# Routing the first half of the tokens ahead of the first mixture of experts, and the rest beside its first nine tiles

## The chip, the cores and the metric

The kernel runs on one core of a Trainium2 chip. The core has a matrix engine (TensorE, PE in the profile, with its weight loads listed as PEld), three engines for elementwise work (VectorE or DVE, ScalarE or ACT, GpSimd or POOL), a queue engine (SyncE or SP) and 16 DMA engines that serve all queues. Matrix products write to PSUM, which has eight banks; everything else lies in SBUF or in DRAM. The metric is the time of one execution on the device in microseconds, less is better. Each engine works through its own instructions strictly in order, so an instruction that waits holds up all that stand behind it on its engine.

## The reference

The reference is a two-layer graph network on 4096 tokens of 256 features, in float32. Each layer adds a graph block and then a mixture of experts to its input `x`:

- Layer 0, graph block: `h = relu(adj @ layernorm(x) @ gcn_w + gcn_b)`, layer-normalised, then a selective state-space block (projection to 2 x 512, a causal convolution of width 4, `silu`, a recurrence over the 4096 tokens with 16 states for each of 512 channels, gating, projection back to 256). The sum with `x` is called x1 here.
- Layer 0, mixture: the tokens of x1 are layer-normalised; a gate of 8 columns with softmax picks the two best experts of each token, with their probabilities as weights; an expert is `gelu(t @ W1 + b1) @ W2 + b2` with 512 hidden units. The reference computes all experts for all tokens and multiplies by weights that are zero but for two; the kernel computes only the two. The sum with x1 is called x2.
- Layer 1, graph block: `tanh(adj * adj)` where `adj > 0`, at most 700 entries a row, times `tanh(layernorm(x2) @ W_proj + b_proj) @ W_gcn`, with bias and relu, added to x2. The sum is called x3.
- Layer 1, mixture: the same scheme with 6 experts of three layers and a router with a hidden layer of 128.

## The kernel before

Tokens are handled in blocks of 128 (`P`), 32 in all (`NT`), and in chunks of four blocks (`CW` = 512 tokens, `TPC` = 4), 8 in all (`NC`). The stages follow each other in the program; within all but the first a scheduler of the language orders each engine's instructions, and may take work of a later stage early where its buffers allow it.

**Graph block of layer 0.** The recurrence runs chunk after chunk; a chunk takes 32 steps, and in each step VectorE does two scans (L1115) and one product (L1125), POOL one product (L1092), ACT two exponentials (L1108), and TensorE adds up over the states (L1142). The order of this part is written out by hand (`tc.manual_schedule`). In the last chunk, beside the recurrence, the class `Norm` reads the finished chunks 0 to 6 of x1 back, normalises them, stores them to the DRAM table `dp.xd` (L945) and computes their gate logits into `lgs` (L964, L970). The class `Last` finishes chunk 7 after the recurrence: `last.norm()` (L1031 to L1066) takes its statistics from PSUM, normalises, transposes, computes logits, and stores x1 of that chunk.

**Routing of the first mixture.** The class `Dispatch` holds it for a mixture. `choose` (through `router`, L108 to L136) makes softmax and the two best experts as one-hot rows. `place` counts with two matrix products (L230, L234) how many assignments of each expert come before, and so gives each assignment a row number, kept as a high part `hi` (row divided by 128) and a low part. `one_hot` writes the low parts as one-hot matrices of 128 columns (L272, eight groups of 128 assignments an instruction; they lie in the buffer of `gn`, free by then). Each expert's rows are padded up to whole tiles of 256 rows (`TR`); with two assignments a token, 8 experts and this padding there are at most `K` = 39 tiles. `tables` turns this round into the list of tokens by row: it adds each expert's first row to `hi`, compares with the number of each half tile (L316), multiplies by group numbers (L321, and on ACT L320), and lets TensorE multiply with the one-hot matrices (L326, 64 products into one PSUM tile). From the sum VectorE derives `src` (which token to fetch, L357), then each tile's expert number `exps`, its bias columns (L364, L370) and `dst` (where to store the result, L387). Tokens are routed in two batches: 24 blocks (chunks 0 to 5) with `dp.choose(0)`, `dp.place(0)` written behind the recurrence, and 8 blocks (chunks 6 and 7) after `last.norm()`. Then `one_hot` for both, one `tables` for all 39 tiles, and after these the tiles.

**Tiles.** `expert_tiles` takes one tile after the other. SP reads the expert number into a register and loads W1 and W2 (512 KB each, three buffers, L493) and the output bias (L496); POOL fetches 256 token rows with two indirect DMAs (L392, four buffers); TensorE transposes (L500), VectorE copies (`xkT`, L504), TensorE does the first layer (L479), ACT the gelu (L483), TensorE the second layer of the tile before (L464), VectorE adds the bias (`yk`, L469), POOL stores the rows with two indirect DMAs to the DRAM table `ys` (L400). 35 tiles are always run, four more only where a count says so (the branch at L1356). Ahead of the tiles SP issues the reload of x1 into the SBUF tile `x2`, chunk by chunk (L1328, 8 x 512 KB), and four loads of layer 1's weights.

**Layer 1.** `combine` reads the results of a chunk back from `ys` and adds them to `x2`; features and propagation follow, and the second mixture, whose routing uses the same `Dispatch`, once for chunks 0 to 5 and once for chunks 6 and 7, each with its own tables. The adjacency tiles of layer 1 are loaded at L1424; the scheduler takes the first eight of these loads, and the elementwise work on them (L1430 to L1437), between tiles of the first mixture.

Of the kernel before, what the change touches and what calls it, by code (L numbers as in the profile page):

```python
# [9 lines left out]
F32 = mybir.dt.float32  # L10
# [8 lines left out]
P = 128  # L19
# [4 lines left out]
TOPK = 700  # L24
SPLIT = 6
# [3 lines left out]
def kernel(ctx: ExitStack, tc: tile.TileContext, out: bass.AP, **a):  # L29
# [131 lines left out]
    class Dispatch:  # L161
# [4 lines left out]
        def __init__(self, pool, E, name, batches, c0=0):  # L166
# [5 lines left out]
            self.C = self.K * TR // P  # L172
# [4 lines left out]
            self.src = pool.tile([P, self.C], I32, name=f"{name}_src")  # L177
            self.dst = pool.tile([P, self.C], I32, name=f"{name}_dst")
# [8 lines left out]
            self.oh, self.runs = [], []  # L187
            for T in sorted(set(batches), reverse=True):
                n = batches.count(T)
                t = pool.tile([P, n, 2 * T + 1, E], BF16, name=f"{name}_oh{T}")  # L190
                nc.gpsimd.memset(t[:, :, :1, :], 0.0)
                self.oh += [t[:, b] for b in range(n)]
                self.runs.append((t, n, T))
# [13 lines left out]
        def start(self):  # L207
            nc.gpsimd.memset(self.count, 0.0)
# [68 lines left out]
        def tables(self, ps, tp, biases, hots=None):  # L277


            E, K, C, name = self.E, self.K, self.C, self.name  # L280
# [6 lines left out]
            base = small.tile([P, 1, E], F32, name="tb_base", bufs=1)  # L287
            nc.vector.tensor_scalar(nt, self.count[:, 0, :], float(TR - 1), None, ALU.add)
            nc.vector.tensor_copy(nti, nt)
            nc.vector.tensor_scalar(nti, nti, TR.bit_length() - 1, None, ALU.arith_shift_right)  # L290
            nc.vector.tensor_copy(nt, nti)
            nc.vector.tensor_tensor_scan(ct[:, 0, :], onesf[:, :E], nt, 0.0, ALU.mult, ALU.add)
            nc.vector.tensor_tensor(base[:, 0, :], ct[:, 0, :], nt, ALU.subtract)
            nc.vector.tensor_scalar(base, base, float(TR // P), None, ALU.mult)
            self.tiles = self.pool.tile([1, 1], F32, name=f"{name}_tiles")
            nc.vector.tensor_copy(self.tiles, ct[0:1, 0, E - 1:E])

            group = self.group.rearrange("p t i -> p (t i)")
            NG = 2 * self.NT
            shift = tp.tile([P, NG], F32, name="tb_shift", bufs=1)  # L300
            g0 = 0
            for oh, n, T in self.runs:
                G, at = 2 * T, shift[:, g0:g0 + 2 * T * n].rearrange("p (n g) -> p n g", n=n)
                one = tp.tile([P, n, G, E], BF16, name=f"tb_one{G}", tag="tb_tmp", bufs=1)
                nc.vector.tensor_tensor(
                    one, oh[:, :, 1:, :], base.unsqueeze(1).to_broadcast([P, n, G, E]), ALU.mult
                )
                nc.vector.tensor_reduce(at, one, AX.X, ALU.add)
                g0 += G * n
            nc.vector.tensor_tensor(shift, shift, self.hi, ALU.add)  # L310
            yield
            S = 2 * TPC
            for g0 in range(0, NG, S):
# [3 lines left out]
                    hot, iota[:, :C].unsqueeze(1).to_broadcast([P, S, C]),  # L317
                    shift[:, g0:g0 + S].unsqueeze(2).to_broadcast([P, S, C]), ALU.is_equal,
# [6 lines left out]
                for g in range(S):  # L325
                    nc.tensor.matmul(  # L326
                        ps[:, :2 * C], self.lo[:, g0 + g, :], eq[:, :2, g, :],
# [4 lines left out]
            tmp = tp.tile([P, K, E], F32, name="tb_tmp", tag="tb_tmp", bufs=1)  # L332
            ge = tp.tile([P, K, E + 1], F32, name="tb_ge", bufs=1)
            ex = tp.tile([P, K], F32, name="tb_ex", bufs=1)
            self.exps = self.pool.tile([P, K], I32, name=f"{name}_exps")
            nc.vector.memset(ge[:, :, 0:1], 1.0)
            nc.vector.tensor_tensor(
                ge[:, :, 1:], iota[:, :K].unsqueeze(2).to_broadcast([P, K, E]),
                ct.to_broadcast([P, K, E]), ALU.is_ge,
            )  # L340
            nc.vector.tensor_reduce(ex, ge[:, :, 1:], AX.X, ALU.add)
            nc.vector.tensor_scalar(ex, ex, float(E - 1), None, ALU.min)
            nc.vector.tensor_copy(self.exps, ex)
            nc.vector.tensor_tensor(ge[:, :, :E], ge[:, :, :E], ge[:, :, 1:], ALU.subtract)
# [8 lines left out]
            nc.vector.tensor_scalar(grp, grp, self.S * TPC - 1, None, ALU.bitwise_and)  # L353
# [4 lines left out]

            yield
            self.bias = []  # L360
            for n, b in enumerate(biases):
                bk = self.pool.tile([P, b.shape[2], K], F32, name=f"{name}_b{n}")
                for m in range(b.shape[2]):
                    mul = nc.vector.tensor_tensor(  # L364
                        tmp, ge[:, :, :E],
                        b[:, :, m].unsqueeze(1).to_broadcast([P, K, E]), ALU.mult,
# [16 lines left out]
                inv[:, 1, :], inv[:, 1, :], float(2 * self.S * CW + TPC - 1), None, ALU.add  # L383
# [3 lines left out]
            nc.vector.tensor_copy(self.dst, tok)  # L387

# [8 lines left out]
        def put(self, k, yk):  # L397
            for j in range(TR // P):
                c = k * (TR // P) + j
                s_ = nc.gpsimd.indirect_dma_start(  # L400
                    out=self.ys[:, :],
# [4 lines left out]
                for o in self.sent[-3:]:  # L406
                    tc.declare_no_dep(s_.ins, o.ins, reason="distinct rows")
                if len(self.sent) > 3:
                    after(s_, self.sent[-4])
                self.sent.append(s_)  # L410
# [1307 lines left out]
```

## Time and profile before

| what | us |
|---|---|
| median of 3 runs | 2433.39 (2431.81 to 2440.27) |
| the profiled execution | 2442.82 |
| its span, first to last instruction | 2440.9 |
| TensorE busy | 2246.4 (92%) |
| VectorE busy | 1642.8 (67%) |
| ScalarE busy | 1194.4 (49%) |
| GpSimd busy | 1144.0 (47%) |
| recurrence's last product on VectorE | 1242 |
| last matrix products of x1 end | 1254 |
| list of tokens written | 1298.5 |
| first tile's transposition | 1302.4 |
| last tile's matrix products end | 1574.4 |

The page of a profile gives each engine's busy time, its busy share in 40 slices of the span, the DMA queues and the costliest groups of instructions. Matrix products are pipelined, so that a busy TensorE need not be at its peak. Other views list the instructions of an engine in order of time, with the idle time ahead of each and what ended it, or add up the busy time of all engines in a given stretch. A tile buffer's numbers are left out of its name.

### The profile page before, as it was taken

To read this page: it belongs to the slowest core of one execution; us is meant where nothing else is said; L and a number is where in the kernel's file an instruction comes from. 1 tells how busy PE (TensorE), PEld (TensorE's weight loads), DVE (VectorE), ACT (ScalarE), POOL (GpSimd) and SP (SyncE) were. 2 spreads that over 40 slices of the span, in tenths; PEclk is the share of its full clock that TensorE was granted. 3 is DMA by queue.
4 is the path that set the end of the run, shared out by engine and by line. 5 is a ranking of instruction groups with operands and counts; after the bars stand their busy time and mean duration, and the time that the engine had idled before them with its cause. 6 is when DMAs were issued, how large, how long until landed. Compare 5 with 4: busy or idle time off the path is not lost. (4 is left out here: it accounts for less than half of the span.)

```text
span 2440.9 us, 27933 instructions
## 1 busy us (share of the span) xinstructions
PE 2246.4 (92%) x8984; PEld 1628.6 (67%) x8984; DVE 1642.8 (67%) x2353; ACT 1194.4 (49%) x2045; POOL 1144.0 (47%) x831
## 2 busy tenths in 40 slices
PE   8999999999999999888966999789999999998985
PEld 7675666556565666544645888667888888877774
DVE  2079999999999999997985211191666667732133
ACT  3255566575755566675733222145555556522221
POOL 1057787777878777765623555310000000145552
PEclk9999999999999999998977999999999999999998
DMA  7289998999999998995746877551444444546686
GB/s 236 87 231 228 249 273 233 276 242 271 246 268 248 255 260 238 272 258 173 245 130 217 252 235 231 160 172 52 147 147 147 147 146 144 164 147 201 215 276 232
DMA packets 290957, 509.46 MB, mean 209 GB/s; under 512 B 25312, under 2 KB 157536, under 8 KB 289904
## 3 DMA queue, kind: packets, MB, share of 16 engines
q1 hardware_dynamic: 244528, 410.54, 53.8%
q0 software_dynamic: 46272, 97.03, 18.5%
q8 instruction: 74, 1.21, 0.2%
q14 instruction: 83, 0.68, 0.1%
HBM read 406.03 MB, written 42.73 MB: 184 GB/s over the span
## 5 line engine op out<-in xcount | busy, mean ns | idle before, releaser
L1092 POOL TENSOR_TENSOR db<-du,bb 128x1024 f32<-128x1024 f32 x256 | 607.6, 2373 | 327.1 <-ACT state L1121 80.0
L1115 DVE TENSOR_TENSOR_SCAN db<-da,state,db 128x512 f32<-128x512 f32 x512 | 627.2, 1266 | 32.2 <-ACT da L1108 30.0
L627 PE MATMUL pt<-at,gn 128*128 128x256 f32 x2048 | 479.7, 387 | 14.9 <-ACT gn L85 9.4
L627 PEld LDWEIGHTS pt<-at,gn 128*128 128x128 f32 x2048 | 396.9, 195 | 137.2 <-issue 62.9
L1108 ACT ACTIVATE da<-dt,negA 128x512 f32<-128x512 f32 x512 | 346.3, 688 | 247.8 <-DVE db L1115 237.2
L1442 PE MATMUL pf<-gn,f 128*128 128x256 f32 x2048 | 452.0, 380 | 0.0
L1442 PEld LDWEIGHTS pf<-gn,f 128*128 128x128 f32 x2048 | 386.6, 190 | 57.2 <-issue 6.4
L1125 DVE TENSOR_TENSOR hc<-db,cb 128x1024 f32<-128x1024 f32 x256 | 327.5, 1279 | 18.1 <-issue 0.4
L1142 PE MATMUL psy<-hc,ident 128*128 128x512 f32 x576 | 304.1, 623 | 4.7 <-DMA hc<-hc 4.6
L469 DVE TENSOR_TENSOR yk<-ps_y,bk 128x512 f32<-128x512 f32 x73 | 50.5, 691 | 341.7 <-PE ps_y L464 273.0
L79 POOL TENSOR_TENSOR ln_rs<-ln_rs,mhalf 128x4 f32<-128x4 f32 (+1 forms) x25 | 33.2, 1330 | 507.1 <-DVE ln_rs L78 506.7
L479 PE MATMUL ps_h<-xkT,wk 128*128 128x256 f32 x864 | 215.2, 390 | 20.6 <-DVE xkT L504 9.4
L1431 ACT ACTIVATE f<-f 128x1024 f32<-128x1024 f32 x128 | 134.6, 1057 | 202.1 <-DVE f L1430 136.8
L464 PE MATMUL ps_y<-wk,hk 128*128 128x256 f32 x864 | 214.6, 385 | 10.5 <-ACT hk L483 6.3
L479 PEld LDWEIGHTS ps_h<-xkT,wk 128*128 128x128 f32 x864 | 160.0, 193 | 57.6 <-ACT hk L483 18.5
L1129 POOL DMA_DIRECT2D hc<-hc x224 | 195.6, 873 | 0.2
L1430 DVE TENSOR_SCALAR f<-at 128x1024 f32<-128x1024 f32 x128 | 88.0, 687 | 149.3 <-PE pf L1442 134.8
L464 PEld LDWEIGHTS ps_y<-wk,hk 128*128 128x128 f32 x864 | 162.9, 193 | 34.0 <-ACT hk L483 7.7
L1142 PEld LDWEIGHTS psy<-hc,ident 128*128 128x128 f32 x576 | 110.5, 198 | 90.8 <-issue 62.1
L1437 DVE SCALAR_TENSOR_TENSOR cnt<-at,cnt 128x1024 bf16<-128x1024 f32 x120 | 146.0, 1217 | 18.4 <-DMA at<-in_adjT_dram 17.7
L483 ACT ACTIVATE hk<-ps_h,d_b 128x256 f32<-128x256 f32 x140 | 65.9, 474 | 185.8 <-PE ps_h L479 171.4
L1432 ACT ACTIVATE f<-f 128x1024 f32<-128x1024 f32 x128 | 134.5, 1055 | 3.4
(306 smaller groups left out, 2550.4 us busy)
## 6 DMA issues: line engine op xcount, KB each, us to landing
at<-in_adjT_dram SPq DMA_DIRECT2D x256, 512.0 KB
bb<-bcd SPq DMA_DIRECT2D x128, 512.0 KB
cb<-bcd SPq DMA_DIRECT2D x128, 512.0 KB
hc<-hc POOLq DMA_DIRECT2D x224, 256.0 KB
wk<-in_L_ffn_W_dram SPq DMA_DIRECT2D x70, 512.0 KB
wk<-in_L_ffn_expert_w_dram SPq DMA_DIRECT2D x114, 256.0 KB
yg<-d_ys SPq DMA_DIRECT2D x14, 512.0 KB
yd<-us SPq DMA_DIRECT2D x6, 1024.0 KB
```

What stands on the lines that cost most here:

```text
L464: nc.tensor.matmul(ps[:, j, :], hT[:, m, j * P:(j + 1) * P], w[:, m, :], start=(m == 0), stop=(m == kb_out - 1),)
L479: nc.tensor.matmul(ps[:, j, :], w[:, d, m * P:(m + 1) * P], xT[:, d, :], start=(d == 0), stop=(d == DB - 1),)
L627: nc.tensor.matmul(pt[:, k, :], xl[:, j, k * P:(k + 1) * P], at[:, jj, :], start=(j == 0 and k == 0), stop=(j == NT - 1 and k == DB - 1),)
L1092: nc.gpsimd.tensor_tensor(self.db, self.f.du[self.half][:, self.mi:self.mi + 1, :].to_broadcast([P, 2, CW]), self.bb, ALU.mult,)
L1108: nc.scalar.activation(da, self.f.dt[self.half][:, self.mi, :], AF.Exp, scale=negA[:, self.m, n:n + 1])
L1115: nc.vector.tensor_tensor_scan(self.db[:, j, :], da, self.db[:, j, :], state[:, self.m, n:n + 1], ALU.mult, ALU.add,)
L1125: nc.vector.tensor_tensor(self.hc, self.db, self.cb, ALU.mult)
L1129: nc.gpsimd.dma_start(self.hc[:, 0, :], self.hc[:, 1, :], accum_op=ALU.add)
L1142: nc.tensor.matmul(f.psy[m], ident, self.hc[:, j, :], start=False, stop=(self.g == GS - 1 and j == last),)
L1431: nc.scalar.activation(f, f, AF.Square)
L1437: nc.vector.scalar_tensor_tensor(cnt, at, 0.0, cnt, ALU.is_gt, ALU.add)
L1442: nc.tensor.matmul(pf[:, t, :], f[:, jj, t * P:(t + 1) * P], gn[:, j, :], start=(j == 0 and t % 2 == 0), stop=(j == NT - 1 and t % 2 == 1),)
```

## The change

The routing of the first mixture is split in two, and the tables are taken out of `Dispatch` into a new class `Part`, which stands for a number of tiles.

- The batches are now 16, 8 and 8 blocks. `dp.choose(0)` and `dp.place(0)` in their old places cover the first half of the tokens (chunks 0 to 3).
- The first `Part` has nine tiles (`FIRST0`), only full ones (`full=True`: each expert's count is divided by 256 and rounded down, and what doesn't fit into nine tiles is left). It is made from the first half alone, right behind `last.norm()`, and its tiles are the first nine. They fetch from a table of their own, `xd0`: the first four normalised chunks are stored twice.
- The second `Part` has the other 30 tiles, of which 26 are always run. Its routing (`others`: choose, place and one-hot for the batches 1 and 2, then the tables over all 64 groups of assignments, less the rows that the first part used) is written in pieces between the first seven tiles, three pieces a tile.
- Layer 1's four loads are written behind tile 7, and the reload of x1 behind tiles 8 to 15, one chunk each. The scheduler may take them earlier.
- Row numbers now carry their expert: the counters start at expert x 8192 instead of 0, `tables` computes a number for each half tile (`slot`) from the expert's base and compares `hi` with it. Layer 1's two tables use the same new code, each as one `Part` over all its tiles. The small work of the tables on tiles and experts stands ahead of the comparisons.
- The routing has one PSUM bank beside the seven of the tiles.

```diff
-        dp = Dispatch(r0, E0, "d0", [NT - 2 * TPC, 2 * TPC])
+        dp = Dispatch(r0, E0, "d0", [NT // 2, 2 * TPC, 2 * TPC])
+
+        xd0 = dram.tile([N // 2, D], F32, name="d0_xdf")
+        part0 = [
+            Part(dp, "d0f", FIRST0, full=True, xd=xd0), Part(dp, "d0r", dp.K - FIRST0, FIRST0)
+        ]
...
                 nc.sync.dma_start(tokens(dp.xd, self.c), self.x)
+                if self.c < NC // 2:
+                    nc.sync.dma_start(tokens(xd0, self.c), self.x)
...
         def start(self):
-            nc.gpsimd.memset(self.count, 0.0)
+            nc.vector.tensor_scalar(
+                self.count[:, 0, :], iota[:, :self.E], float(SPAN), None, ALU.mult
+            )
...
+            nc.vector.scalar_tensor_tensor(
+                nt, iota[:, :E], -float(SPAN), dp.count[:, 0, :], ALU.mult, ALU.add
+            )
+            if not self.full:
+                nc.vector.tensor_scalar(nt, nt, float(TR - 1), None, ALU.add)
             nc.vector.tensor_copy(nti, nt)
             nc.vector.tensor_scalar(nti, nti, TR.bit_length() - 1, None, ALU.arith_shift_right)
             nc.vector.tensor_copy(nt, nti)
+            if other is not None:
+                nc.vector.tensor_tensor(nt, nt, other.used[:, :E], ALU.subtract)
...
                 nc.vector.tensor_tensor(
-                    hot, iota[:, :C].unsqueeze(1).to_broadcast([P, S, C]),
-                    shift[:, g0:g0 + S].unsqueeze(2).to_broadcast([P, S, C]), ALU.is_equal,
+                    hot, slots, dp.hi[:, g0:g0 + S].unsqueeze(2).to_broadcast([P, S, C]),
+                    ALU.is_equal,
                 )
...
+            if self.full:
+                u = self.used[:, :E]
+                nc.vector.tensor_scalar(u, base, -1.0, float(F), ALU.mult, ALU.add)
+                nc.vector.tensor_scalar(u, u, 0.0, None, ALU.max)
+                nc.vector.tensor_tensor(u, u, nt, ALU.min)
...
-                dp.choose(1, lgs[:, dp.T[0]:, :], gate_b, False, ra)
-                dp.place(1, ps_r, "pl", ra)
-                for b in range(2):
-                    dp.one_hot(b)
-                b1 = load(wp, a["L0_ffn_b1"], "b1")
-                for _ in dp.tables(ps_r.tile([P, CW], F32, name="ps_inv", tag="pl"), rp, [b1]):
-                    pass
-            early.close()
-            for c in range(NC):
-                nc.sync.dma_start(x2[:, c * TPC:(c + 1) * TPC, :], tokens(x1d[c], 0))
...
+            b1 = load(wp, a["L0_ffn_b1"], "b1")
+            dp.one_hot(0)
+            for _ in part0[0].tables(inverse(), rp, [b1], NT):
+                pass
+
+            def others():
+                for b in (1, 2):
+                    t0 = dp.t0[b]
+                    dp.choose(b, lgs[:, t0:t0 + dp.T[b], :], gate_b, False, rp)
+                    yield
+                    dp.place(b, ps_r, "pl", rp)
+                    yield
+                    dp.one_hot(b)
+                    yield
+                yield from part0[1].tables(inverse(), rp, [b1], 2 * NT, part0[0])
+
+            def then0(n):
+                if n < FIRST0 - 2:
+                    for _ in range(3):
+                        next(pieces, None)
+                elif n == FIRST0 - 2:
+                    assert next(pieces, None) is None
+                    loads.append(load_bcast(keep, a["L1_gnn_b_gcn_row"], "b_gcn_b"))
+                    loads.append(load(wp, a["L1_gnn_W_proj"], "w_proj"))
+                    loads.append(load(wp, a["L1_gnn_b_proj"], "b_proj"))
+                    loads.append(load(wp, a["L1_gnn_W_gcn"], "w_gcn"))
+                elif n < FIRST0 - 1 + NC:
+                    c = n - FIRST0 + 1
+                    nc.sync.dma_start(x2[:, c * TPC:(c + 1) * TPC, :], tokens(x1d[c], 0))
...
-            most0 = 2 * N // TR + dp.E // 2 - 1
+            most0 = 2 * N // TR + dp.E // 2 - 1 - FIRST0
+            tiles0(
+                [(part0[0], k) for k in range(FIRST0)] + [(part0[1], k) for k in range(most0)],
+                then0,
+            )
```

## The prediction

> **What bounds the kernel now.** The page's slices come first: TensorE (PE) is at 8 or 9 tenths everywhere but around 1220 to 1340 us. I then asked for that stretch by stage. Columns: stretch, its length, busy time of PE, PE weight loads, VectorE (DVE), ScalarE (ACT) and GpSimd (POOL), granted PE clock, busy share of the DMA engines, GB/s.
>
> ```profile
> 1150.00:1205.00 55.00, 53.51 (x221) 35.86 (x220) 52.79 (x47) 41.49 (x114) 36.38 (x16) 0.97 0.76 238
> 1270.00:1290.00 20.00, 3.61 (x24) 2.80 (x25) 18.73 (x59) 3.09 (x4) 0.00 (x0) 0.50 0.95 299
> 1330.00:1350.00 20.00, 16.30 (x77) 13.17 (x75) 9.37 (x13) 10.74 (x16) 10.21 (x10) 1.00 0.97 329
> 1365.00:1560.00 195.00, 194.96 (x952) 167.94 (x951) 33.96 (x53) 50.14 (x106) 100.40 (x102) 1.00 0.75 229
> ```
>
> In the scan (first row) VectorE has no room left. Between scan and mixture (second row) PE stands still, at clock 0.50, while VectorE routes. In the steady mixture (last row) PE is full and VectorE idles five sixths of the time. So routing is paid for where PE is idle and could lie where VectorE is idle. VectorE in order of time (start, duration, instruction, idle before and releaser) shows the path:
>
> ```profile
> 1231.92 2.45 DVE L1115 TENSOR_TENSOR_SCAN db<-da,state,db 128x512 f32<-128x512 f32 x2
> 1234.29 0.42 DVE L108 TENSOR_TENSOR rt_lg<-lgs,gate_b 128x192 f32<-128x192 f32 x1
> 1235.77 2.44 DVE L1115 TENSOR_TENSOR_SCAN db<-da,state,db 128x512 f32<-128x512 f32 x2
> ...
> 1253.28 0.76 DVE L1031 BATCH_NORM_STATS2 ln_st<-ps_out 128x6 f32<-128x256 f32 x2 [1.25 <-PE ps_out L1017]
> 1261.52 2.35 DVE L272 TENSOR_TENSOR gn<-iota,pl_row 128x1024 bf16<-128x1024 f32 x2
> 1284.08 1.53 DVE L316 TENSOR_TENSOR tb_eq<-iota,tb_shift 128x624 bf16<-128x624 f32 x2
> 1296.75 0.32 DVE L351 COPY tb_inv<-ps_inv 128x156 f32<-128x156 f32 x1 [1.00 <-PE ps_inv L326]
> 1298.32 0.20 DVE L357 CAST d_src<-tb_tok 128x78 int32<-128x78 f32 x1
> 1321.62 0.69 DVE L469 TENSOR_TENSOR yk<-ps_y,bk 128x512 f32<-128x512 f32 x1 [13.70 <-PE ps_y L464]
> 1348.85 1.22 DVE L1437 SCALAR_TENSOR_TENSOR cnt<-at,cnt 128x1024 bf16<-128x1024 f32 x1 [4.18 <-DMA at<-in_adjT_dram]
> 1556.19 0.69 DVE L469 TENSOR_TENSOR yk<-ps_y,bk 128x512 f32<-128x512 f32 x1 [6.08 <-PE ps_y L464]
> ```
>
> From the last normalisation's first instruction (1253.28) to the list of tokens (1298.52) VectorE works 45.2 us almost without a gap. PE in order of time shows what follows:
>
> ```profile
> 1302.43 0.47 PE L500 MATMUL ps_xt<-ident,xk 128*128 128x128 f32 x1 [5.72 <-DMA xk<-d_xd,d_src]
> 1322.97 3.75 PE L479 MATMUL ps_h<-xkT,wk 128*128 128x256 f32 x16
> 1358.34 3.65 PE L479 MATMUL ps_h<-xkT,wk 128*128 128x256 f32 x16
> 1365.72 3.65 PE L479 MATMUL ps_h<-xkT,wk 128*128 128x256 f32 x16
> 1568.59 5.78 PE L464 MATMUL ps_y<-wk,hk 128*128 128x256 f32 x26
> 2089.36 0.57 PE L326 MATMUL pf<-tb_eq,d_lo 128*128 128x116 bf16 x8
> ```
>
> The first transposition comes 3.9 us after the list, the period is 7.38 us (1358.34 to 1365.72), the 35th tile ends at 1574.4. Whatever starts the tiles earlier moves that end, less what PE itself is given to do.
>
> **The change, part by part.** The first half of the tokens has 4096 assignments over 8 experts, so at least (4096 - 8 x 255)/256 = 8.03 full tiles: nine always exist, and 9 + 26 is again 35 tiles.
>
> *Scan.* Choosing for 16 blocks needs only the first four chunks' logits; in the built order it stands eight steps before the scan's end, 17 instructions among scans where three stood. The rows above bound one: a step with one is 3.85 us (1231.92 to 1235.77), without 3.69 (the spacing of the neighbouring steps). Single ones add 0.1 to 0.16; where three or four stand together each adds its 0.3 (rows of 0.23 at 64 elements and 0.36 at 192). Sum 4.5, less 0.3 for the three of before: +4. Ends: 0 (a 1.47 us wait for ACT at 1212.42 lies there) and 17 x 0.36 = 6.1. ACT's copy of the last logits hangs on the scans, so PE shifts along.
>
> *From 1253.28 to the list.* New sum: placing 16 blocks with the normalisation's statistics 8.3 (8.24 before; 1.1 less for shorter rows, 1.2 more for nine small ones put among them); four one-hot blocks at 1.21, 4.9 (of eight, the other four go beside the tiles); twenty small ones 4.6 (14 took 3.2 at 1280.85); eight comparisons and products over 144 elements at 0.25 (0.37 at 208, 0.80 at 624), five router instructions at 0.25 and one `f` of 0.69, 4.0; a wait for PE of 0.4; sixteen to the list at 0.2, 3.2. Together 25.4 against 45.2: -19.8. Ends: 23 and 30, if dependent neighbours pay 0.26 each.
>
> That `f` is a new wait: the first adjacency tile of the next layer, loaded behind the last x1 stores (1267.14 and 1.11 us, plus the 4), with everything to the list queued behind it on VectorE. An uncrowded such load took about 2.7 us (issued 1330.97, used 1333.62), so it lands near 1276; VectorE gets there near 1278. Cost 0; ends 0 and 3.
>
> The first tile's fetches and weights need only the new list and expert numbers; the 3.9 us stay. The start moves by -19.8 + 4 = **-15.8** (ends -22 and -9).
>
> *PE beside the tiles.* The second table's 64 matrix products over 120 columns and one placement move from an idle PE into a full one. 0.57/8 = 0.071 us each at full clock gives 4.6, the placement 0.4: **+5.0**; at half clock 9.5.
>
> *VectorE beside the tiles.* About 40 us of routing: four one-hot blocks 4.9, sixteen comparisons and products over 480 elements at 0.64 (the 464-element row) 10.2, bias tables 5.5, some 80 small ones at 0.23. Room: 13.70 idle in the fill and 6.08 in each of six tiles, 50 us. It fits, but an in-order queue puts a tile's copy behind it. Following both built orders, tile 3's `xkT` copy comes 1.4 us late and the first table products wait 0.8 for VectorE: **+2.5**. Ends 0 and 8.5 (40 plus six tiles' own 1.38 each, without the fill).
>
> *x1 reload and layer 1's weights.* 4.85 MB leave the idle stretch (1270 to 1290, 299 GB/s) and stand on SP between the weights of tiles 3 to 6. Free there: 329 - 229 = 100 GB/s over 30 us, 3.0 MB; the remaining 1.85 MB is 5.6 us at 329. Weights are fetched two tiles, 14.8 us, ahead, which covers most: **+0.5**, ends 0 and 5.6. What SP no longer does ahead of the weights (7.38 us of x1 issues) is part of the start above.
>
> *Copy of the first four normalised chunks.* 2.1 MB more writes within 1150 to 1205, where a quarter of 55 us is free, enough for 4 MB at 299: 0. No wait of POOL for a `bb` load is in that stretch, which is the cover; without it 2.1 MB at 238 GB/s, 8.8 us.
>
> *Next layer's adjacency prefetch.* Seven of its eight loads now come at tiles 10 to 12; the 4.18 us wait at 1348.85, with `yk` and `xkT` behind it, should recur: 0, ends -4.2 and +4. Layer 1's tables change by a few short instructions beside 16 us of matrix products a chunk: 0, ends -1 and +1.
>
> A rule bears on POOL. Its indirect DMAs are slower beside VectorE:
>
> ```profile
> 1310.96 0.95 POOL L392 DMA_INDIRECT xk<-d_xd,d_src  x1 [0.30 <-issue]
> 1342.96 1.44 POOL L392 DMA_INDIRECT xk<-d_xd,d_src  x1 [0.30 <-issue]
> ```
>
> Four a tile at 1.44 + 0.30 are 7.0 us, still under 7.38, so I add nothing. The Trainium skill, SBUF — State Buffer, section "Who interferes with whom", says that VectorE in a two-port mode shuts GpSimd out for the whole instruction. By that rule, with VectorE twice as busy, each of four could wait for another copy of some 0.69 us and a tile would take up to 9.7: six tiles, 14 us more, and no gain.
>
> **Sum.** -15.8 + 5.0 + 2.5 + 0.5 = **-7.8 us**. The profiled execution took 2442.8 (span 2440.9), giving 2435.0; the median of the runs shown, 2433.39, lies 9.4 lower, so I predict **2425.6**.
>
> **Rivals.**
> - *More is kept* (2419, net -14): the tables' matrix products fall into PE gaps of the fill and tile copies are not late. For it: 20.5 us for the first two tiles (1302.43 to 1322.97) against 14.8. Against: in the built order the products stand at tiles 3 to 5, after the fill. With the adjacency wait gone too, -19.
> - *VectorE's queue holds the tiles* (2445, +12): every one of tiles 1 to 5 waits some 4 us for `yk` or `xkT` behind routing, 20 us in place of 2.5; -7.8 - 2.5 + 20 = +9.7, +12 with half a microsecond more a tile. For it: 40 of 50 us, and at 1348.85 one blocked VectorE instruction cost PE a tile's slack. Against: two PSUM buffers before the copy. It decides from 10.3 us of such waits on.
> - *The bus* (2434, about 0): copy and reload cost 8 together. Against: shares of 0.76.
> - That nine tiles aren't full, so that more tiles would be run, is excluded above.
>
> **How the numbers follow.** Forecast (-3 to -13) 0.44; more kept 0.26; VectorE's queue 0.20; bus 0.10. A measurement of this kernel tells about 0.5% (12.2 us) from no change. Faster by more: 0.26 and 0.06 of the forecast, 0.32. Slower by more: 0.14 of the queue's and 0.04 of the bus's, 0.18. Within: 0.50. Range -19 to +10: 2414 to 2443; the forecast's own 2420 to 2430.
>
> **What would show it.** First transposition near 1286; the scan's end 4 us later; the list 25 us after the last statistics begin; table products at 0.07 each; tiles 3 to 5 at 9 to 10 us, then 7.38; last tile's end near 1566. It is wrong if the list is late behind `f`, if `yk` waits for routing, or if scans wait for `bb`.

## The result, and the profile after

On the same chip, in four executions each, the kernel before took 2433.01 us (2431.81 to 2440.27) and the changed kernel 2413.25 us (2411.92 to 2416.96). The ratio is 0.9912, with a 95% interval of 0.9895 to 0.9929: about 20 us faster. The forecast was 2425.6 with a gain of 7.8; its sign was right, its size was not, and 2413.25 lies just below the range, which began at 2414.

The windows of the changed kernel (columns as in the prediction):

```profile
1150.00:1205.00 55.00, 53.52 (x219) 36.05 (x218) 52.18 (x46) 41.58 (x108) 35.64 (x16) 0.97 0.85 279
1270.00:1290.00 20.00, 7.76 (x50) 5.51 (x51) 12.27 (x70) 5.35 (x9) 10.61 (x11) 0.50 0.85 271
1380.00:1545.00 165.00, 165.00 (x807) 142.38 (x806) 29.41 (x46) 41.98 (x89) 82.25 (x84) 1.00 0.73 221
```

"The bus" stands here for the 16 DMA engines together. In the scan it is busier (0.76 before, 0.85 now) and VectorE is not (52.8 and 52.2 us): the extra copy is seen, and a run below shows that it costs nothing. In the stretch where PE stood still for 16.4 of 20 us, its idle part is down to 12.2. The steady mixture is as full as it was.

VectorE in order of time, from the recurrence's last product to the list:

```profile
1245.63 1.23 DVE L1171 TENSOR_TENSOR hc<-db,cb 128x1024 f32<-128x1024 f32 x1
1255.15 0.76 DVE L1077 BATCH_NORM_STATS2 ln_st<-ps_out 128x6 f32<-128x256 f32 x2 [1.90 <-PE ps_out L1063]
1262.36 4.62 DVE L273 TENSOR_TENSOR gn<-iota,pl_row 128x1024 bf16<-128x1024 f32 x4
1266.90 0.23 DVE L324 TENSOR_TENSOR tb_ge<-iota,tb_ct 128x72 f32<-128x72 f32 x1
1267.04 0.16 DVE L335 SCALAR_TENSOR_TENSOR tb_coef<-tb_base,tb_coef 128x8 f32<-128x8 f32 x1
1267.12 0.13 DVE L419 COPY d0f_tiles<-tb_ct 1x1 f32<-1x1 f32 x1
1269.33 0.53 DVE L359 TENSOR_TENSOR tb_eq<-tb_slot,d_hi 128x144 bf16<-128x144 f32 x2
1273.08 0.69 DVE L1504 TENSOR_SCALAR f<-at 128x1024 f32<-128x1024 f32 x1 [1.16 <-DMA at<-in_adjT_dram]
1273.68 0.19 DVE L381 COPY tb_inv<-ps_inv 128x36 f32<-128x36 f32 x1
1275.21 0.17 DVE L387 CAST d0f_src<-tb_tok 128x18 int32<-128x18 f32 x1
```

From the first statistics (1255.15) to the list (1275.38) it is 20.2 us, against 45.2 before and 25.4 forecast. The starts of three small neighbours, 1266.90, 1267.04 and 1267.12, show the main reason: they are 0.14 and 0.08 us apart, where the forecast paid 0.2 and more. The `f` of the next layer's adjacency does stand ahead of the list, and it waits.

PE in order of time, from the first tile's transposition on:

```profile
1283.01 0.48 PE L539 MATMUL ps_xt<-ident,xk 128*128 128x128 f32 x1 [5.98 <-DMA xk<-d_xdf,d0f_src]
1312.67 1.00 PE L369 MATMUL ps_inv<-tb_eq,gn 128*128 128x120 bf16 x16
1315.73 1.42 PE L369 MATMUL ps_inv<-tb_eq,gn 128*128 128x120 bf16 x24
1324.76 1.42 PE L369 MATMUL ps_inv<-tb_eq,gn 128*128 128x120 bf16 x24
1335.11 3.65 PE L518 MATMUL ps_h<-xkT,wk 128*128 128x256 f32 x16
1547.04 5.78 PE L503 MATMUL ps_y<-wk,hk 128*128 128x256 f32 x26
```

The first transposition is 7.6 us behind the list (3.9 before), the second table's 64 products take 3.84 us between tiles 3 to 5, and the last tile ends at 1552.8, 21.6 earlier. From there to the end it takes 857.9 us; the profile shown of before had 866.5 there.

### The profile page after: what moved, and what is told of

It is laid out like the page before. It is cut to its first block, busy times and chain, and to the rows that moved or that the text cites. A ratio compares the mean times of both kernels' runs of the same rounds, so it can differ in the third digit from the quotient of the medians.

```text
span 2410.7 us, 28097 instructions
## 1 busy us (share of the span) xinstructions
PE 2239.3 (93%) x9018; PEld 1624.2 (67%) x9018; DVE 1648.1 (68%) x2455; ACT 1194.8 (50%) x2050; POOL 1144.8 (47%) x828
## 5 line engine op out<-in xcount | busy, mean ns | idle before, releaser
L518 PE MATMUL ps_h<-xkT,wk 128*128 128x256 f32 x864 | 213.6, 388 | 14.7 <-DVE xkT L543 6.9
L787 PE MATMUL ps_xz<-hT,w_in 128*128 128x512 f32 x256 | 116.3, 597 | 15.2 <-ACT hT L771 8.8
```

The lines of the kernel that those rows point to most:

```text
L518: nc.tensor.matmul(ps[:, j, :], w[:, d, m * P:(m + 1) * P], xT[:, d, :], start=(d == 0), stop=(d == DB - 1),)
```

## The experiments

The runs were made in four groups, each on one chip; the kernel before takes 2436 us on one of these chips and 2418 to 2420 on the others, so totals are compared within a group. Places in time are measured from the first statistics of the last normalisation ("S"), since the recurrence ahead of it ends some us earlier or later from execution to execution. "S to end" is the time to the end of the last tile's products: 297.7 in the profile above, 321.1 in that of before.

**A second profile of before**, the kernel unedited.

> The kernel of before, unchanged, for a second profile. The profiled execution shown before took 2442.8 us, 9.4 over the median. Theory 'path' (the whole gain lies ahead of the last tile): the last tile's products end near 1574 again, and from there to the end it is about 858 us, as after the change, not 866.5. Theory 'rest' (the new layer-1 tables, written in the same way, save some 8 us behind the tiles): 866 again, and the last tile ends about 9 us earlier than 1574. For the end of the recurrence: the 12 last additions over states on PE took 8.19 us in the profile shown; if that is what this stage costs, 8 again; if it is a matter of the clock granted in that execution, about 5.4.

2438.1 us. The last tile ends at 324.5 from S and the rest takes 859.4, so theory "path" holds: in the four profiles made on this chip the rest is 859 to 862, in the twelve of the other groups 844 to 850, for old and new code alike. The 866.5 was therefore most likely a matter of that one execution, which also took 9.4 us more than the median. The twelve additions took 7.09 us here; this is taken up below.

**All routing written ahead of the tiles.**

```diff
             pieces, loads = others(), []
+            for _ in pieces:
+                pass
```

> The changed kernel, with all the routing of the second half run on VectorE ahead of the first tile (the pieces are no longer written between the tiles). Theory 'path': the list of the first tiles is still there near 1275, but VectorE then has about 40 us of routing ahead of the first copy of a tile, so the first layer of tile 0 starts near 1310 to 1315 in place of 1287; tiles 3 to 5 then run at 7.4 us, which gives back 3.5. Net 20 to 25 us slower than the changed kernel, 2433 to 2438. Rival 'other causes' (bus, adjacency and clock carry the gain, not the order of the routing): within 6 us of the changed kernel, below 2420.

2426.07, ratio 0.9957 (0.9935 to 0.9979), S to end 310.0: slower than the changed kernel, but by some 10 us and not by the 20 to 25 that were expected. The place in the text is not the place in the queue: the scheduler put the tiles' copies between the pieces again, so this is not the experiment it was meant to be. A later run does it with a dependency.

**x1's reload and layer 1's loads put back ahead of the tiles.**

```diff
             pieces, loads = others(), []
+            for c in range(NC):
+                nc.sync.dma_start(x2[:, c * TPC:(c + 1) * TPC, :], tokens(x1d[c], 0))
+            loads.append(load_bcast(keep, a["L1_gnn_b_gcn_row"], "b_gcn_b"))
...
-                    loads.append(load_bcast(keep, a["L1_gnn_b_gcn_row"], "b_gcn_b"))
...
-                    nc.sync.dma_start(x2[:, c * TPC:(c + 1) * TPC, :], tokens(x1d[c], 0))
```

> The changed kernel, with the reload of x1 and the four loads for layer 1 (4.85 MB) issued ahead of the first tile's weights, as before the change. At 299 GB/s they hold the bus 16 us from about 1270 on, so the first tile's weights land near 1290 instead of 1280. Theory 'path': with a list at 1275 the reload is no longer covered by routing, and tile 0's first layer starts 4 to 9 us later than 1287; 2417 to 2422. Rival (the bus never mattered, only VectorE's path): 2413, no difference.

2428.47, ratio 0.9975 (0.9964 to 0.9987), S to end 313.5. That is 14 us more than the mean of the changed kernel's three profiles, which were made on other chips; against the next run, on the same chip, it is 10.3 more (303.2), and the time is 11 us longer. So 10 to 14 us of the gain are lost, more than either theory said. Its windows:

```profile
1270.00:1290.00 20.00, 6.08 (x18) 3.00 (x19) 12.72 (x67) 3.40 (x3) 12.66 (x13) 0.50 1.03 339
1290.00:1310.00 20.00, 14.57 (x34) 10.51 (x34) 13.26 (x49) 4.87 (x10) 3.38 (x4) 0.59 0.64 211
```

The bus is full in the first stretch, and PE runs at clock 0.59 in the second. A second profile of the changed kernel has there:

```profile
1270.00:1290.00 20.00, 9.44 (x35) 7.02 (x36) 13.26 (x70) 5.63 (x8) 12.03 (x12) 0.60 0.76 253
1290.00:1310.00 20.00, 20.00 (x109) 16.99 (x108) 14.12 (x48) 6.70 (x15) 8.88 (x8) 1.00 0.91 279
```

Tile 0's first layer starts 39.2 us after S instead of 31.9, which is 7.3 of them. The rest goes with late tiles at a low clock, with routing queued ahead of their activations, as ScalarE's row in the run with the reload ahead shows:

```profile
1303.22 1.28 ACT L363 ACTIVATE tb_eq<-tb_eq,part 128x480 bf16<-128x480 bf16 x2 [6.31 <-DVE tb_eq L359]
1304.40 1.18 ACT L522 ACTIVATE hk<-ps_h,d0f_b 128x256 f32<-128x256 f32 x3
```

ScalarE waited 6.31 us for VectorE's comparison, the tile's `hk` stood behind it, and PE idled 3.95 us for `hk`. This is the rival in which a queue holds the tiles; it needed late weights to appear.

**Without the second copy of four chunks.**

```diff
-            Part(dp, "d0f", FIRST0, full=True, xd=xd0), Part(dp, "d0r", dp.K - FIRST0, FIRST0)
+            Part(dp, "d0f", FIRST0, full=True), Part(dp, "d0r", dp.K - FIRST0, FIRST0)
...
-                if self.c < NC // 2:
-                    nc.sync.dma_start(tokens(xd0, self.c), self.x)
```

> The changed kernel without the second copy of the first four normalised chunks: the first nine tiles fetch from the one table, behind its last store, which is issued at 1262.4. 2.1 MB less is written beside the recurrence. Theory 'copy is free': the recurrence ends within 0.5 us of where it did, and the last store has long landed when the list is there at 1275, so 2413 +- 2. Rival (the copy holds up the recurrence or the bus): up to 8 us faster, 2405.

2417.22, ratio 0.9914 (0.9895 to 0.9932), as for the changed kernel; VectorE ends the recurrence at 1245.4, where the mean over all kernels with the new scan is 1245.3. The copy is free; and since the first fetch comes at the same place without it, it isn't needed either.

**The changed kernel again, the adjacency loads moved, the first fetch moved, and both**, on one chip. The second edit:

```diff
+                if c == 0 and j2 < 4:
+                    after(ld, dp.sent[-1])
```

The third (`fetched` collects the fetches):

```diff
                 ld = nc.sync.dma_start(w, src(e))
+                if 0 < len(fetched) - 1 < 3:
+                    after(ld, fetched[0])
```

> The changed kernel itself, beside the next three on the same chip. From the first statistics of the last normalisation to the end of the last tile's products 297.7 us in its first profile, the list of tokens 20.2 after the statistics, the first transposition 27.9, tile 3 54.4. Theory 'path': these recur within 1 us; the 5 to 6 us by which such stretches of different executions differ lie in the tiles 9 to 12, at the adjacency prefetch. 2413 to 2417.

> The changed kernel, with the first eight loads of layer 1's adjacency made to wait for the last tile's results, so that none of that work lies between tiles. It removes the wait of 1.16 us ahead of the list and the stall of 2.0 us at tiles 9 and 10; 3.2 us off VectorE and ACT work there is done later, in the features stage, where TensorE waits for nothing of it. Theory 'adjacency matters': the list comes 19 us after the statistics instead of 20.2, tiles 9 to 12 run at 7.38 and the last tile ends 3 us earlier, 2410 to 2413; but the eight loads with their elementwise work (8 times 0.69 + 1.22 on VectorE) now stand ahead of the propagation, which may give it all back. Rival 'it is only moved': no difference in the total, 2413 to 2417, with the last tile 3 us earlier and the stage behind it 3 us longer.

> The changed kernel, with the weights of tiles 1 and 2 ordered behind the first tile's fetch (tile 0's weights stay where they were). In the changed kernel the first transposition comes 7.6 us behind the list in place of 3.9, with three tiles' weights issued between 1270.85 and 1277.7 and a DMA share of 0.91. Theory 'the fetch queues behind the weights': list to first transposition falls to 4 to 5 us, the last tile ends 3 us earlier, about 2411. Rival (6 us is what such a fetch takes when started so early, for the descriptors or the new table): it stays at 7.6, and tiles 1 and 2 come later, 2414 to 2420.

> The two edits together: adjacency loads behind the tiles, and the weights of tiles 1 and 2 behind the first fetch. Sum of the two if they are independent: 6 us less than the changed kernel, about 2408. If the stage behind the tiles gives the adjacency part back: 2411.

| kernel | us | ratio to before (interval) | S to list | list to transposition | S to end |
|---|---|---|---|---|---|
| changed, again | 2401.11 | 0.9921 (0.9904 to 0.9938) | 20.3 | 8.1 | 301.8 |
| adjacency behind the tiles | 2396.53 | 0.9909 (0.9892 to 0.9926) | 18.6 | 8.0 | 294.1 |
| first fetch ahead of weights | 2400.57 | 0.9915 (0.9897 to 0.9934) | 20.3 | 4.0 | 305.6 |
| both | 2396.08 | 0.9905 (0.9888 to 0.9922) | 18.6 | 3.9 | 294.1 |

In the changed kernel's second profile the list and the first transposition come where they did (20.3 and 28.4 us after S, 20.2 and 27.9 in the first), and the stretch is longer at the prefetch: two tiles take 8.1 and 13.7 us there, 7.6 and 9.1 in the first profile.

The fetch did queue behind three tiles' weights: with the weights of tiles 1 and 2 behind it, the 3.9 us of before are back. But that is worth nothing in the total, and up to the last tile it is 3.8 us worse. PE in the third kernel:

```profile
1276.09 0.48 PE L544 MATMUL ps_xt<-ident,xk 128*128 128x128 f32 x1 [2.31 <-DMA xk<-d_xdf,d0f_src]
1281.76 0.90 PE L544 MATMUL ps_xt<-ident,xk 128*128 128x128 f32 x3 [2.48 <-DMA xk<-d_xdf,d0f_src]
1289.30 7.03 PE L520 MATMUL ps_h<-xkT,wk 128*128 128x256 f32 x24
1300.08 3.66 PE L520 MATMUL ps_h<-xkT,wk 128*128 128x256 f32 x16
```

Tile 1's fetch now stands behind the weights instead, and tile 2 starts 48.2 us after S where it was 46.1. A likely reason, not tried by itself, is that the bytes ahead of tile 2 are the same in any order. Moving the adjacency takes 7.7 us out of the stretch to the last tile (5.4 against the mean of the three profiles); in the total the intervals overlap.

**The adjacency moved in the kernel before; all routing ahead of the first fetch; 24 more small instructions**, on another chip. The second edit holds back the first nine tiles' fetches (`last` is the second part's cast of its destinations):

```diff
+                if self.full:
+                    after(got, self.other.last)
```

The third and the fourth stand ahead of `d0f_src`:

```diff
+            for _ in range(24 if self.full else 0):
+                nc.vector.tensor_scalar(tok, tok, 0.0, None, ALU.add)
```

```diff
+            alone = [
+                nc.vector.tensor_scalar(pad[:, i, :], tok, 0.0, None, ALU.add)
+                for i in range(24 if self.full else 0)
+            ]
```

> The kernel of before, with the first eight adjacency loads of layer 1 made to wait for the last tile's results, as in adj_late. It prices the prefetch without the change. Rival 'adjacency' (the change gains because the prefetch stalls the tiles less: 5.9 us in before, 2.0 after): then before gains 6 or more from this edit alone, 0.9975 or less, where the changed kernel gained 4.6 (2396.5 against 2401.1), and what is left of the change between the two kernels without prefetch shrinks to about 15. Theory 'path': before gains about as much as the changed kernel, 5 +- 2, the change keeps 17 to 20 us without any prefetch, and from the first statistics of the last normalisation to the last tile's end it takes 315 us in place of 321 to 324 (294.1 in adj_late).

2416.11 against 2418.05, ratio 0.9992 (0.9981 to 1.0003), S to end 312.4: in the total less than either theory gave it, up to the last tile more. The square below takes this up.

> The changed kernel, with the first tiles' fetches made to wait for the whole routing of the second half too (the destination list of the second part). Nothing of the routing then lies beside tiles. Theory 'path': the second part's list stands near 35 us behind the first one's, so the first transposition comes 55 to 60 us after the statistics in place of 28, the tiles run at 7.4 us from the start (3.4 given back) and the adjacency is loaded by then; 24 to 28 us slower than the changed kernel, 5 to 9 slower than before. Rival 'the new way of computing the tables is cheaper in itself' (and the order matters little): between the changed kernel and before.

2422.02, ratio 1.0015 (1.0002 to 1.0028), S to end 323.9, which is 24.4 more than the mean of 299.5 of three profiles of the changed kernel. The time is 4.0 us longer than that of before, a little less than "path" gave. PE in this kernel:

```profile
1309.44 0.47 PE L541 MATMUL ps_xt<-ident,xk 128*128 128x128 f32 x1 [9.90 <-DMA xk<-d_xdf,d0f_src]
1333.54 0.60 PE L541 MATMUL ps_xt<-ident,xk 128*128 128x128 f32 x4
1340.91 0.60 PE L541 MATMUL ps_xt<-ident,xk 128*128 128x128 f32 x4
1348.29 0.60 PE L541 MATMUL ps_xt<-ident,xk 128*128 128x128 f32 x4
```

The first transposition comes 60.2 us after S and the tiles run at 7.37 from then on. The rival gave a time between the two kernels and falls: the new way of computing the tables saves nothing in itself, and the whole gain (and more) hangs on what lies beside the tiles.

> The changed kernel, with 24 more instructions on 18 elements ahead of the list, each adding zero to the result of the one before, with pieces of the other batches' routing put between them by the scheduler. By the price in the forecast (0.2 us each) the list comes 4.8 us later, 25.0 after the statistics. Theory 'a dependent instruction costs 0.2, and what is put between is covered': the same 4.8, with the other pieces between them costing nothing of their own. If only the issue counts (0.08 each, with 0.13 for what stands between): 2 to 5.

> The changed kernel, with 24 more instructions on 18 elements ahead of the list that need nothing of each other, one behind the other. By the forecast's price of 0.2 us: 4.8 later. Theory 'instructions that don't wait for each other are 0.08 apart' (as the neighbours in the changed kernel's list): 1.9 later, 22.1 after the statistics.

These two were executed once each, 2403.72 us with the dependent and 2405.72 with the independent ones, which is too few to compare totals; what they tell is in the rows. VectorE with 24 independent instructions:

```profile
1272.62 1.96 DVE L389 TENSOR_SCALAR tb_pad<-tb_tok 128x18 f32<-128x18 f32 x24
1274.62 0.17 DVE L392 CAST d0f_src<-tb_tok 128x18 int32<-128x18 f32 x1
```

Each costs 0.082 us and the list comes 2.1 later (22.4 after S): as the theory said. With 24 dependent ones the list comes 8.8 us later (29.1), more than any theory said. A piece of it:

```profile
1272.16 0.17 DVE L388 TENSOR_SCALAR tb_tok<-tb_tok 128x18 f32<-128x18 f32 x1
1272.25 0.22 DVE L123 TENSOR_TENSOR rt_p<-rt_lg,rt_red 128x64 f32<-128x64 f32 x1
1272.38 0.17 DVE L388 TENSOR_SCALAR tb_tok<-tb_tok 128x18 f32<-128x18 f32 x1
1277.58 1.22 DVE L273 TENSOR_TENSOR gn<-iota,pl_row 128x1024 bf16<-128x1024 f32 x1
1278.71 0.17 DVE L388 TENSOR_SCALAR tb_tok<-tb_tok 128x18 f32<-128x18 f32 x1
```

A link of the chain is 0.20 to 0.22 us from the next with one small piece of other routing between them, and that piece is free. Larger pieces are not: between some links the scheduler put pieces of 0.28 to 0.69 us, and between the last ones two one-hot blocks of 1.22. That work is done then, and the last tile ends 304.1 after S, 4.5 behind the mean of the changed kernel's profiles, though the list is 8.8 later.

**The square.** Both kernels with the prefetch between the tiles and behind them, four kernels on one chip; the edits are those above.

> First corner of a square on one chip: the kernel of before, with the prefetch of the adjacency between its tiles. Theory 'path': from the first statistics of the last normalisation to the last tile's end 315 to 325 us, of it 3 to 9 at the prefetch; ratio to the kernel before 1.000.

> Second corner: the kernel of before with the prefetch behind the tiles. 312.4 us from the statistics to the last tile's end, as in the first run of it. In total 2 to 5 us faster than the first corner.

> Third corner: the changed kernel with the prefetch between its tiles. 17 to 20 us faster than the first corner. If the prefetch carried part of the gain, this difference is larger by 3 us or more than that between the second and the fourth corner.

> Fourth corner: the changed kernel with the prefetch behind the tiles. 294 us from the statistics to the last tile's end. Theory 'path': 17 to 20 us faster than the second corner. Rival 'adjacency': 15 or less faster than the second corner.

| | prefetch between tiles | prefetch behind them |
|---|---|---|
| before: us, ratio | 2421.25, 1.0003 (0.9990 to 1.0017) | 2415.57, 0.9983 (0.9971 to 0.9996) |
| changed: us, ratio | 2398.90, 0.9914 (0.9895 to 0.9934) | 2398.99, 0.9917 (0.9900 to 0.9933) |
| before: S to end | 321.0 | 313.7 |
| changed: S to end | 299.2 | 294.5 |

The change is worth 22.4 us with the prefetch and 16.6 without, in S to end 21.8 and 19.2. The 16.6 lies just below what "path" gave and above what "adjacency" gave: the shorter path carries most of the gain, the prefetch 3 to 6 us of it. The intervals reach 3 to 5 us to either side, so the totals alone don't settle the prefetch's share; over all profiles the S to end differs by 22.7 us with the prefetch and 18.8 without, which makes the share 3.9. PE's transpositions of tiles 3 to 6 in before, with the prefetch between them:

```profile
1323.30 0.60 PE L500 MATMUL ps_xt<-ident,xk 128*128 128x128 f32 x4
1334.96 0.60 PE L500 MATMUL ps_xt<-ident,xk 128*128 128x128 f32 x4
1342.56 0.60 PE L500 MATMUL ps_xt<-ident,xk 128*128 128x128 f32 x4
1353.75 0.60 PE L500 MATMUL ps_xt<-ident,xk 128*128 128x128 f32 x4
```

The steps are 11.66, 7.60 and 11.19 us. VectorE's wait in the second long one:

```profile
1344.30 1.23 DVE L1437 SCALAR_TENSOR_TENSOR cnt<-at,cnt 128x1024 bf16<-128x1024 f32 x1 [4.38 <-DMA at<-in_adjT_dram]
```

In the changed kernel the long steps are two of 8.72 and 9.85:

```profile
1346.62 0.60 PE L539 MATMUL ps_xt<-ident,xk 128*128 128x128 f32 x4
1355.34 0.60 PE L539 MATMUL ps_xt<-ident,xk 128*128 128x128 f32 x4
1365.19 0.60 PE L539 MATMUL ps_xt<-ident,xk 128*128 128x128 f32 x4
```

For the changed kernel the moved prefetch gained 4.6 us on one chip and nothing on the other, where the rest after the last tile took 850.4 instead of 846.1. That it beats the changed kernel is not settled.

## Why the prediction was right or wrong, point by point

Means over the three profiles of each of the two kernels, in us; the first row is from all eighteen profiles, and the last two steps are set apart by the two profiles of each kernel with the prefetch moved away.

| step | forecast | measured |
|---|---|---|
| scan: start of the statistics | +4 | +0.1 (1252.3 in five profiles with the old scan, 1252.4 in thirteen with the new) |
| statistics to list | -19.8 | -25.1 (45.4 to 20.3) |
| list to first transposition | 0 | +4.2 (3.9 to 8.1) |
| routing and reload beside the tiles | +8.0 | +3.9 (transposition to end, prefetch moved away: 263.6 to 267.5) |
| adjacency prefetch between the tiles | 0 | -5.6 (9.3 to 3.7) |
| sum | -7.8 (with layer 1 at 0) | -22.5 |

The timed gains are 20, 17 and 22 us on three chips; the recurrence and the rest behind the tiles differ from execution to execution by as much as the distance to 22.5.

The mechanism stood, and the sum was short by 14.7 us because five of its steps were mis-sized. Four gave too little gain: the price of small VectorE instructions between the statistics and the list (by 5.3), the prefetch put at 0 (5.6), the routing and reload beside the tiles (4.1) and the scan (3.9). One gave too much: the first fetch's 3.9 us, which were to stay (4.2). No one of them explains the miss alone.

- **Which path it was: right.** The list starts the tiles, PE runs through from there, and with the routing put back on that path the gain is gone. No tiles were added (35 run in every profile).
- **From the statistics to the list: too dear by 5.3.** What failed here is the price of small instructions: "twenty small ones 4.6" took 2.4 and "sixteen to the list at 0.2, 3.2" took 1.7, 3.7 of the 5.3; placing took 7.2 for 8.3, and the one-hot blocks 4.5 for 4.9. The first price was the mean of thirteen rows from 1280.85 on, seven of which read 128 to 384 elements, where the new ones read 72 at most; the second was a duration, while the ten instructions that end the old list start 0.17 us apart on average (1296.75 to 1298.32), and the sixteen that end the new one 0.10. With other work between dependent neighbours, an independent instruction took 0.08 us of the queue, and the pieces of the second half's routing, which the forecast put beside the tiles, filled the gaps.
- **`f`: cost 0 was wrong, the bound of 3 right.** It waits 1.16 and runs 0.69; with the adjacency moved, the list comes 1.7 us earlier.
- **The scan: a cost that was not there.** VectorE ends its last product 2.2 us later on average (1243.1 and 1245.3, same eighteen profiles), but the ends lie up to 5 us apart within one kind. The last twelve steps, which hold all the choosing, tell it better: 48.4 to 48.5 us in all five profiles with the old scan, 49.9 in all thirteen with the new, so the choosing costs 1.4 us more, a third of the forecast. A wait for ACT that was there before took up part of it (1.47 us in the profile of before, 0.61 in that of the changed kernel). The statistics don't move, since PE is quicker behind it. PE's twelve last additions over states, in the second profile of before and of the changed kernel:

```profile
1242.60 7.09 PE L1142 MATMUL psy<-hc,ident 128*128 128x512 f32 x12
```

```profile
1243.80 5.40 PE L1188 MATMUL psy<-hc,ident 128*128 128x512 f32 x12
```

They took 6.84 to 8.19 us in all five profiles with the old scan, at a mean granted clock of 0.66 to 0.79 over them; with the new one 5.40 at a clock of 1.00 in ten of thirteen, 7.09 at 0.76 in three. The low clock is a stretch of 3.4 or 6.8 us at 0.50. With the old scan it begins 1 to 2 us after a wait of PE of 1.42 us, in all five; with the new one, where PE waits 1.2 us and mostly once more 1.4, such a stretch comes in six of thirteen, and in three of these it lies ahead of the last additions. So this part of the gain is luck as far as the forecast goes. The Trainium skill, TensorE: Matmul & The Clock Gate, section "Part 1: The HAM clock gate (the "warmup" mystery)", says that the clock is halved until a window of activity, whose phase runs freely, has been busy; a low clock of some us at varying places agrees with that. Why the new scan meets it here less often was not tried.

- **List to transposition: 0 was wrong by 4.2, for the worse.** The forecast said that "fetches and weights need only the new list and expert numbers; the 3.9 us stay", and did not price what is on the bus when the fetch starts. In both kernels SP sends three tiles' weights once the expert numbers are there, ahead of the fetch. Before, the numbers were ready 15.0 us ahead of the list (L343, 1283.37), and between 1298 and 1300, when the first fetch starts, the bus was busy 0.09 of the time. Now they are ready 7.3 us ahead (L389, 1267.95), and from 1276 to 1278 the share is 0.96. The last of the weights and the first fetch, before and after:

```profile
1289.04 1.26 SPq L493 DMA_DIRECT2D wk<-in_L_ffn_W_dram  x2
1299.49 1.10 POOL L392 DMA_INDIRECT xk<-d_xd,d_src  x1 [39.69 <-DVE tb_tok L375]
```

```profile
1275.37 1.60 SPq L532 DMA_DIRECT2D wk<-in_L_ffn_W_dram  x2
1276.34 1.18 POOL L430 DMA_INDIRECT xk<-d_xdf,d0f_src  x1 [15.75 <-DVE d_oh L133]
```

With the weights moved, the wait comes back at tile 2.

- **PE beside the tiles: +5.0 was +3.9.** 64 products at 0.060 us are 3.84. Nothing else is lost there. PE's transpositions of tiles 3 to 6 in the fourth corner:

```profile
1305.64 0.60 PE L539 MATMUL ps_xt<-ident,xk 128*128 128x128 f32 x4
1315.23 0.61 PE L539 MATMUL ps_xt<-ident,xk 128*128 128x128 f32 x4
1324.28 0.61 PE L539 MATMUL ps_xt<-ident,xk 128*128 128x128 f32 x4
1331.63 0.60 PE L539 MATMUL ps_xt<-ident,xk 128*128 128x128 f32 x4
```

The spacing is 9.59, 9.05 and then 7.35 to 7.38. So VectorE's +2.5 and the reload's +0.5 were 0, and no placement shows: one of the two falls into the idle PE ahead of the first tile, the other into the fill. (The upper end of 8.5 for VectorE does not follow from the numbers beside it: 48.3 us of work in six periods of 7.38 leaves 4.0.) The rival with VectorE's queue fell, though the reload run shows what it would look like.

- **The prefetch: "should recur" was half wrong.** It recurs later and costs less. Both sizes vary: 8.3, 11.2 and 8.3 in before against the profiles without it, 2.3, 5.9 and 2.8 after. The bound of -4.2 was set by one wait; PE lost more than that, because other steps were stretched too.
- **The extra copy at 0: right.** So was layer 1 at 0, as far as the rest behind the tiles tells it: 844 to 850 us on three chips, on two of them with both kernels.
- **GpSimd.** By the rule in the Trainium skill, SBUF — State Buffer, section "Who interferes with whom", up to 9.7 us were estimated for each of six tiles, and no gain. POOL's row that is longest while the second table is made is

```profile
1318.78 1.42 POOL L439 DMA_INDIRECT d_ys<-yk,d0f_dst  x1 [0.30 <-issue]
```

which is no longer than the 1.44 of before. With the prefetch moved away only the two tiles with table products are long, and those products account for it, so the rows decide against the estimate here.

In all, the number of the rival "more is kept", with the adjacency wait gone too (-19), lies nearest, and it had a chance of 0.26. Its mechanism was right in half: tile copies were not late and the prefetch cost less, but the table products stood beside tiles 3 to 5 and took 3.84 us, where the rival had them fall into gaps of the fill. That the number fits is partly luck, since the cheaper list, the cheaper scan and the longer fetch belong to no rival. The range ended at -19, without room for terms that were too dear by themselves.

## What to carry to other kernels

Price a chain of small VectorE instructions twice: by the spacing of dependent ones (0.2 us here), and by that of independent ones (0.08) where other work can be put between them; moving work into those gaps can be free. A path that is shortened uncovers what was hidden behind it: here the reload of x1, harmless behind 45 us of routing, cost 10 to 14 us behind 20, so the loads had to be moved with the routing. When the order matters, use a dependency: the place in the program text did not decide the queue.

## What was not expected of the hardware

The same kernel's recurrence ends up to 3 us earlier or later from execution to execution, and the part of the kernel behind the first mixture takes 859 to 862 us on one chip and 844 to 850 on others; both are as large as several terms of the sum. The first tile was transposed 3.9 to 4.0 us after its list in the kernel before, where the bus was nearly idle at the fetch (a share of 0.09), and where only one tile's weights went ahead of the fetch; it took 7.3 to 8.5 us where more loads of 512 KB were still under way (0.96 in the changed kernel).
